# A graph layer with attention on one NeuronCore: a fifth gather buffer, block 0's messages during the setup, and 1 / sqrt by Newton's steps on VectorE

## The chip, the cores and the metric

The program runs on one core of a Trainium2 chip. The metric is the device time of one execution in microseconds; before the change it is 1334.2 us, the median of 8 runs (1331.74 to 1335.88). A profile is one such execution with every instruction's start, duration and semaphores recorded. PE is TensorE, with its weight loads shown as PEld; DVE is VectorE, ACT ScalarE, POOL GpSimd, SP SyncE.

## The reference, cut to what matters

There are 8192 nodes of 256 features, in groups of 32, and 131072 edges sorted by their target, with 64 attributes each. All data is fp32.

```python
ea  = edge_attr @ w_e + b_e                       # 131072 x 256
msg = relu(x[src] + ea)
agg = segment_sum(msg, dst, num_segments=8192)    # dst is sorted
h_local = bn(relu((x + agg) @ w1 + b1) @ w2 + b2 + x)
# attention with 4 heads of 64 inside each group of 32 nodes
h_attn  = bn(softmax(q k^T / 8) v @ out_w.T + out_b + x)
out = h_local + h_attn
out = bn(out + relu(out @ m_w1 + m_b1) @ m_w2 + m_b2)
return layernorm(x + out)                         # (z - mean) / sqrt(var + 1e-5)
```

## The kernel before, in words

**Edges** go in 128 blocks of 1024. A block's source rows come by `gather` (L133): eight indirect DMAs of 128 rows of 1 KB each, issued by POOL (L138), into one buffer `xs` of a ring of four. The first 20 blocks (`NX`) read x itself, and a matmul with `sel` and `be` adds the edge bias (L462). Later blocks read `xb`, a copy of x with the bias added; the copy is made in 13 pieces while the first blocks run: load `xp` (L551), add `be` on DVE (L556), store (L557), all loads and stores from SP's queue. Indices of blocks 0 and 1 are loaded directly (`srcd`, L64); those of the others are turned by PE in the setup (L196) and copied to `srci` (L197).

Per block, `edge_products` (L454) multiplies the attributes, transposed on DVE (L164), by `w_e` into two PSUM tiles `pe` (L468). `edge_messages` (L479) adds the gathered rows on DVE (L488) and applies Relu on ACT (L489). `edge_hot` (L494) makes one-hot rows of the target's place; `edge_sums` (L508) sums messages by a matmul with them; `edge_place` (L526, L536) puts the sums into the transposed nodes `xT` of the right chunk.

**Nodes** go in 16 chunks of 512. `attention_front` loads x (L279), transposes it (L286) and makes q and k (L297). `attention_back` makes v (L311), the scores (L328, into the same two PSUM tiles as the edge products), a softmax on DVE and ACT (L344 to L355, Exp at L346), the values (L363) and the output projection (L375). `dense` runs four matmul layers (all at L394, called from L401, L404, L410 and L419), transposes back (L431), and ends with the layer norm: statistics per row (L436, L437), Sqrt on ACT (L439), a reciprocal (L442), the scaling (L444) and the store (L447). Chunks 0 to 13 run as one `dense` call each; 14 and 15 are cut in five smaller calls.

**What sets the order.** PE's order is written out by the program. The main loop takes blocks in pairs up to `TAIL` = 104: gather for two blocks ahead, products and messages of the first, sums of the pair before, a share of node work, products and messages of the second, placing, another share, one-hots, and the rest. `Work.run` hands out the node work: four streams (BACK, FRONT, DENSE, DENSE2) of generators that yield the cost they put on PE; a stream goes on when its `ready` condition holds. A pair has the budget 2 x `PER` (2 x `PER_X` for the first 20 blocks), given in shares of 0.2, 0.2 and 0.6. BACK may make scores only when no products wait for their messages. From block 104 on a second loop places each step by expected times: block i's gather is taken to come at 11.5 + 10.06 (i + 1) us. DVE's and ACT's order is that of the program up to block 26 (`NV`), then a scheduler's. POOL issues the gathers in block order; before a gather its buffer must have been read by the messages of four blocks earlier.

Of the kernel before, what the change touches and what calls it, by code (L numbers as in the profile page):

```python
# [9 lines left out]
FP = mybir.dt.float32  # L10
I32 = mybir.dt.int32
# [13 lines left out]
NH = 4  # L25
# [20 lines left out]
LN_EPS = 1e-5  # L46
REST = -1.0
# [6 lines left out]
def gnn_kernel(ctx: ExitStack, tc: tile.TileContext, x, src, dst, edge_attr, w, out):  # L54
# [37 lines left out]
    be = const.tile([P, TJ, C], FP, name="be")  # L92
# [40 lines left out]
    def gather(b):  # L133
        xs = epool.tile([P, NH, TJ, C], FP, name="xs", tag="xs", bufs=4)
        for h in range(NH):
            for j in range(TJ):
                idx = srcd[:, b * NH + h, j : j + 1] if b < ND else srci[:, b, h * TJ + j : h * TJ + j + 1]
                nc.gpsimd.indirect_dma_start(  # L138
                    out=xs[:, h, j, :],
                    out_offset=None,  # L140
                    in_=x if b < NX else xb[:, :],
                    in_offset=bass.IndirectOffsetOnAxis(ap=idx, axis=0),
                )
        xs_of[b] = xs
# [9 lines left out]
    load_edges(0)  # L154
    gather(1)
    load_edges(1)
# [8 lines left out]

    with tc.tile_pool(name="setup", bufs=1) as sp:


        srci_r = npool.tile([P, BE], I32, name="srci_r", tag="y")
        dsti_r = npool.tile([P, BE], I32, name="dsti_r", tag="h1")  # L170
        nc.sync.dma_start(srci_r, src.rearrange("(s e) -> s e", s=NB))
        nc.sync.dma_start(dsti_r, dst.rearrange("(s e) -> s e", s=NB))
        for h in range(NH):
            nc.scalar.dma_start(we[h * QR : (h + 1) * QR], w["w_e"].rearrange("(i d) c -> d i c", d=QR))
        nc.scalar.dma_start(be, w["b_e"][None, None, :].to_broadcast([P, TJ, C]))
        in_r = npool.tile([P, 3 * KC, C], FP, name="in_r", tag="m1")
        out_r = npool.tile([P, KC, C], FP, name="out_r", tag="vn")
        nc.scalar.dma_start(in_r, w["in_w"].rearrange("(o p) c -> p o c", p=P))
# [4 lines left out]
        nc.scalar.dma_start(out_r, w["out_w"].rearrange("(o p) c -> p o c", p=P))  # L183
        for b in range(2):
            edge_transpose(b)
            load_edges(b + 2)
# [6 lines left out]
        for h in range(NH):  # L193
# [3 lines left out]
            nc.vector.tensor_copy(srci[:, :, h * TJ : (h + 1) * TJ].rearrange("p s j -> p j s"), ps)  # L197

# [78 lines left out]
    def attention_front(n0, st, pool, bank):  # L277
        xn = st["xn"] = pool.tile([P, TN, C], FP, name="xn", tag="xn", bufs=4)
        nc.sync.dma_start(xn, x[ds(n0, CH), :].rearrange("(t p) c -> p t c", p=P))  # L279
        yield REST  # L280
# [102 lines left out]

    def dense(n0, st, pool, bank, t_a=0, t_z=TN, own=("h1", "m1", "zT", "y", "")):
# [54 lines left out]
        nc.scalar.activation(rstd[:, :nt], mv[:, :nt, 1], AF.Sqrt, bias=eps_t)  # L439
        st["dense"] = t_z == TN  # L440
        yield 0.9 * part
        nc.vector.reciprocal(rstd[:, :nt], rstd[:, :nt])  # L442
# [7 lines left out]

    chunk = [{} for _ in range(NCH)]
    pe_of, msg_of, oh_of, newest = {}, {}, {}, {}

    def edge_products(b):  # L454

        eaT = eaT_of.pop(b).rearrange("p t m r -> p t (m r)")
        pes = [bank2().rearrange("p i (j c) -> p i j c", j=TJ) for _ in range(2)]
        pe_of[b, 0], pe_of[b, 2] = pes
        quarter = [slice(h * QR, (h + 1) * QR) for h in range(NH)]
        if b < NX:  # L460
            for h, rows in enumerate(quarter):
                nc.tensor.matmul(  # L462
                    pes[h // 2][:, h % 2], sel[rows, :], be[rows], start=True, stop=False, skip_group_check=True
                )
        for j in range(TJ):
            for i in range(ED // QR):
                for h, rows in enumerate(quarter):
                    nc.tensor.matmul(  # L468
                        pes[h // 2][:, h % 2, j, :], eaT[rows, j * ED // QR + i, :], we[rows, i, :],
                        start=(b >= NX and i == 0), stop=(i == 1), skip_group_check=True,  # L470
                    )

    def next_edges(b):
        if b < NB:
            edge_transpose(b)
        if b + 2 < NB:
            load_edges(b + 2)

    def edge_messages(b):  # L479

        xs = xs_of.pop(b)
        msg = msg_of[b] = epool.tile([P, NH, TJ, C], FP, name="msg", tag="msg", bufs=3)
        n = 2 if b < NB - 1 else 1
        for h in range(0, NH, 2):
            pe = pe_of.pop((b, h))
            for u in range(0, 2, n):
                hs = slice(h + u, h + u + n)
                nc.vector.tensor_add(msg[:, hs], pe[:, u : u + n], xs[:, hs])  # L488
                nc.scalar.activation(msg[:, hs], msg[:, hs], AF.Relu)  # L489

    def edge_hot(b):

        oh = oh_of[b] = epool.tile([P, TB, WN], FP, name="oh", tag="oh", bufs=2)
        nc.vector.tensor_tensor(  # L494
            oh,
            iota_n[:, None, :WN].to_broadcast([P, TB, WN]),
            rel[:, b, :, None].to_broadcast([P, TB, WN]),
            ALU.is_equal,
        )

    def edge_sums(blocks):

        pw = pps.tile([P, 2, C], FP, name="pw", tag="pw", bufs=1)
        for i, b in enumerate(blocks):
            msg, oh = msg_of.pop(b), oh_of.pop(b)
            for j in range(TJ):
                for h in range(NH):
                    nc.tensor.matmul(  # L508
                        pw[h * WN : (h + 1) * WN, i, :], oh[:, h * TJ + j, :], msg[:, h, j, :],
                        start=(j == 0), stop=(j == TJ - 1), skip_group_check=True,  # L510
                    )
        n = len(blocks)
        ws = epool.tile([P, 2, C], FP, name="ws", tag="ws", bufs=2)
        newest["ws"] = nc.scalar.copy(ws[:, :n], pw[:, :n]).ins  # L514
        oh2 = epool.tile([P, 2, WB], FP, name="oh2", tag="oh2")
        for i, b in enumerate(blocks):
            nc.vector.tensor_scalar(oh2[:, i, :], iota_n, wrow[:, b : b + 1], None, ALU.is_equal)
        return blocks, ws, oh2

    def edge_place(blocks, ws, oh2):  # L520

        l2 = pps.tile([P, KC, C], FP, name="l2", tag="pw", bufs=1)
        last = len(blocks) - 1
        for i in range(last + 1):
            for k in range(KC):
                nc.tensor.matmul(  # L526
                    l2[:, k, i * NPB : i * NPB + WB], ws[:, i, k * P : (k + 1) * P], oh2[:, i, :],
                    start=(i == 0 and k == 0), stop=(i == last), skip_group_check=True,
                )
        n = blocks[0] * NPB - WL  # L530
        end = n + last * NPB + WB
        for c in range(max(n, 0) // CH, (min(end, N) - 1) // CH + 1):
            assert chunk[c]["v"]
            a, z = max(n, c * CH), min(end, (c + 1) * CH)
            xT = chunk[c]["xT"][:, :, a - c * CH : z - c * CH]
            newest["xT"] = nc.vector.tensor_add(xT, l2[:, :, a - n : z - n], xT).ins  # L536
# [330 lines left out]
```

## Time and profile before

| what | value |
|---|---|
| median of 8 runs, lowest, highest | 1334.2, 1331.74, 1335.88 us |
| the profiled execution's own time | 1332.63 us |
| its span, first to last instruction | 1330.8 us |
| mean granted TensorE clock | 0.966 |
| POOL: first gather starts, last ends | 4.13, 1299.66 us |
| ACT: table loads | 22 of 1283 ns (11 before Sqrt, 10 before Exp, 1 at the start) |
| DVE: additions for xb (L556) | 13, 18.4 us |
| DMA | 207 MB, 156 GB/s on average |

How to read it: the page gives each engine's busy time as a share of the span. Matmuls are pipelined, so a PE share of 90% does not say that PE sets the end. Groups of instructions carry, after the first bar, busy time and mean duration of one in ns, and after the second the idle time just before them with what ended it; "issue" means that nothing in the profile held the engine. In a timeline a row has start, duration, engine, line, operation, what is written and read, and how many instructions are merged. The table by stage gives for each stretch its length, then busy time of PE, PEld, DVE, ACT and POOL with counts, the granted clock, the DMA share and GB/s.

### The profile page before, as it was taken

Reading aid. Unit: us, or ns where it says so; the run is one execution under the profiler, and the core shown is the slowest. Engines: PE = TensorE matmul, PEld = TensorE weight load, DVE = VectorE, ACT = ScalarE, POOL = GpSimd, SP = SyncE. Lnnn points to the kernel's source line nnn. Section 1 sums busy time; section 2 is a strip of 40 time slices with the busy share of each in tenths; the row PEclk is TensorE's granted clock in tenths of the full one; section 3 lists DMA queues with packets and bytes.
Section 4 is the critical chain, followed back from the end, with each engine's and each line's share of the span. In section 5 each row is a group of like instructions: output and inputs, shape, how many; then the busy total and the mean of one; then the engine's idle time right before and its main releaser. Section 6 shows DMA issues by size and latency. Waiting matters only on the chain.

```text
span 1330.8 us, 24244 instructions
## 1 busy us (share of the span) xinstructions
PE 1210.1 (91%) x9683; PEld 738.8 (56%) x9683; DVE 784.9 (59%) x1347; ACT 586.3 (44%) x840; POOL 984.7 (74%) x1032
## 2 busy tenths in 40 slices
PE   4998989998989989899998979999897998979987
PEld 3565645555555545555555545555555555545755
DVE  5676655746565564746646564665746467464754
ACT  2434344454535444454535435453544536343433
POOL 6777777777777777777777777777777777777770
PEclk9998989999999989999898999999998999989989
DMA  8887654545454454545545454554545445454540
GB/s 272 273 264 275 187 174 137 153 144 162 136 150 140 136 151 138 162 135 145 152 135 155 137 151 139 142 156 136 158 131 158 132 137 160 127 145 130 161 122 30
DMA packets 92882, 207.23 MB, mean 156 GB/s; under 512 B 20798, under 2 KB 39772, under 8 KB 91996
## 3 DMA queue, kind: packets, MB, share of 16 engines
q0 software_dynamic: 49152, 134.28, 35.3%
q1 hardware_dynamic: 41388, 69.76, 16.2%
q10 hardware_dynamic: 2224, 1.58, 0.5%
q8 instruction: 78, 1.28, 0.4%
q14 instruction: 40, 0.33, 0.1%
HBM read 188.77 MB, written 16.78 MB: 154 GB/s over the span
## 4 chain that ended last, share of the span: by engine, by line
PE 59%; POOL 11%; DVE 11%; issue 8%; DMA 5%; ACT 5%; DVEq 0%; ACTq 0%; SPq 0%; POOLq 0%
PE at L394 19%; PE pe L468 14%; POOL xs L138 11%; PE at L297 7%; PE pw L508 6%; DVE msg L488 4%; PE l L526 4%; PE at L375 4%; PE at L311 3%; DMA xs<-xb,srci 2%; ACT msg L489 1%; ACT pr L338 1%; DMA xs<-in_x_dram,srci 1%; PE at L363 1%; DVE eaT L164 1%
## 5 line engine op out<-in xcount | busy, mean ns | idle before, releaser
L138 POOL DMA_INDIRECT xs<-xb,srci x864 | 824.3, 954 | 263.4 <-issue 244.8
L489 ACT ACTIVATE msg<-msg 128x1024 f32<-128x1024 f32 (+1 forms) x258 | 270.0, 1050 | 456.1 <-DVE msg L488 451.0
L488 DVE TENSOR_TENSOR msg<-pe,xs 128x1024 f32<-128x1024 f32 (+1 forms) x258 | 305.0, 1196 | 153.1 <-PE pe L468 70.1
L468 PE MATMUL pe<-we,eaT 32*128 32x256 f32 x4096 | 291.3, 402 | 31.4 <-DVE msg L488 17.5
L468 PEld LDWEIGHTS pe<-we,eaT 32*128 32x128 f32 x4096 | 222.5, 193 | 121.6 <-issue 68.7
L138 POOL DMA_INDIRECT xs<-in_x_dram,srci x144 | 143.9, 999 | 43.9 <-issue 40.2
L164 DVE STREAM_TRANSPOSE eaT<-ea 128x512 f32<-128x512 f32 x128 | 90.1, 704 | 105.1 <-PE pe L468 102.4
L508 PE MATMUL pw<-msg,oh 128*32 128x256 f32 x2048 | 127.7, 385 | 0.0
L394 PE MATMUL at<-hA,mw 128*128 128x512 f32 (+2 forms) x304 | 123.8, 533 | 2.6 <-ACT oT L370 1.8
L297 PE MATMUL at<-xT,inT 128*128 128x512 f32 x256 | 124.8, 613 | 0.2 <-ACT xT L287 0.2
L394 PE MATMUL at<-m,mw 128*128 128x512 f32 (+2 forms) x304 | 117.3, 528 | 0.3
L508 PEld LDWEIGHTS pw<-msg,oh 128*32 128x32 f32 x2048 | 59.1, 110 | 61.8 <-issue 26.6
L526 PE MATMUL l<-oh,ws 128*128 128x160 f32 x512 | 90.6, 316 | 2.8 <-ACT ws L514 2.8
L526 PEld LDWEIGHTS l<-oh,ws 128*128 128x128 f32 x512 | 73.3, 192 | 28.2 <-issue 21.3
L394 PEld LDWEIGHTS at<-hA,mw 128*128 128x128 f32 x304 | 53.2, 190 | 52.1 <-issue 42.0
L394 PEld LDWEIGHTS at<-m,mw 128*128 128x128 f32 x304 | 54.4, 190 | 48.3 <-issue 44.2
L297 PEld LDWEIGHTS at<-xT,inT 128*128 128x128 f32 x256 | 47.2, 193 | 53.7 <-issue 48.2
L394 PE MATMUL at<-h,w 128*128 128x512 f32 (+2 forms) x152 | 67.0, 567 | 7.7 <-ACT h L401 6.7
L394 PE MATMUL at<-xT,w 128*128 128x512 f32 (+2 forms) x152 | 66.8, 577 | 6.6 <-DVE xT L536 6.6
L300 ACT ACTIVATE qk<-at,vec 128x512 f32<-128x512 f32 x64 | 43.4, 681 | 56.9 <-PE at L297 56.8
L419 DVE SCALAR_TENSOR_TENSOR zT<-at,s,zT 128x512 f32<-128x512 f32 (+2 forms) x38 | 25.2, 664 | 66.0 <-PE at L394 65.4
L378 DVE SCALAR_TENSOR_TENSOR hA<-at,s,hA 128x512 f32<-128x512 f32 x32 | 24.0, 750 | 67.7 <-PE at L375 67.7
(107 smaller groups left out, 1209.3 us busy)
## 6 DMA issues: line engine op xcount, KB each, us to landing
ea<-in_edge_attr_dram SPq DMA_DIRECT2D x128, 256.0 KB
xs<-xb,srci POOLq DMA_INDIRECT x864
xn<-in_x_dram SPq DMA_DIRECT2D x16, 512.0 KB
out_dram<-y SPq DMA_DIRECT2D x14, 512.0 KB
xp<-in_x_dram SPq DMA_DIRECT2D x10, 512.0 KB
xb<-xp SPq DMA_DIRECT2D x10, 512.0 KB
xp<-in_x_dram SPq DMA_DIRECT2D x3, 1024.0 KB
xb<-xp SPq DMA_DIRECT2D x3, 1024.0 KB
```

Of the source, the lines that this page charges most:

```text
L138: nc.gpsimd.indirect_dma_start(out=xs[:, h, j, :], out_offset=None, in_=x if b < NX else xb[:, :], in_offset=bass.IndirectOffsetOnAxis(ap= ...
L164: nc.vector.transpose(eaT, ea.rearrange("p (m t d) -> p t m d", m=EQ, d=QR))
L297: nc.tensor.matmul(ps, inT[:, k, o * P : (o + 1) * P], xT[:, k, :], start=(k == 0), stop=(k == KC - 1))
L300: nc.scalar.activation(qk[:, o, :], ps, AF.Identity, bias=v_("in_b", o))
L311: nc.tensor.matmul(ps[:, (t - t0) * C : (t - t0 + 1) * C], xT[:, k, t * P : (t + 1) * P], inT[:, k, 2 * C :], start=(k == 0), stop=(k == K ...
L375: nc.tensor.matmul(ps, outT[:, k, o * P : (o + 1) * P], oT[:, k, :], start=(k == 0), stop=(k == KC - 1))
L394: nc.tensor.matmul(ps, wt[:, k, o * P : (o + 1) * P], act[:, k, :], start=(k == 0), stop=(k == nk - 1))
L468: nc.tensor.matmul(pes[h // 2][:, h % 2, j, :], eaT[rows, j * ED // QR + i, :], we[rows, i, :], start=(b >= NX and i == 0), stop=(i == 1), ...
L488: nc.vector.tensor_add(msg[:, hs], pe[:, u : u + n], xs[:, hs])
L489: nc.scalar.activation(msg[:, hs], msg[:, hs], AF.Relu)
L508: nc.tensor.matmul(pw[h * WN : (h + 1) * WN, i, :], oh[:, h * TJ + j, :], msg[:, h, j, :], start=(j == 0), stop=(j == TJ - 1), skip_group_ ...
L526: nc.tensor.matmul(l2[:, k, i * NPB : i * NPB + WB], ws[:, i, k * P : (k + 1) * P], oh2[:, i, :], start=(i == 0 and k == 0), stop=(i == la ...
```

## The change: a fifth buffer, a new setup order, Newton's steps, and the planner's numbers

Seven things change.

1. `xs` has five buffers in place of four. The bias tile `be` holds one row of 256 in place of two, and is broadcast where it is read.
2. In the setup all loads but the first index loads go by SP's queue: indices, edges of block 0, `w_e`, edges of block 1, the bias, targets, twelve vectors, `in_w`, x of chunk 0, `out_w`, x of chunk 1. Before, `w_e`, the bias, `in_w` and `out_w` were issued by ACT, and x came later.
3. Block 0's products, its next edges and its messages are made inside the setup, after the source indices are turned and ahead of the transposes of `in_w`; the main loop then leaves them out for block 0.
4. In `dense` calls of a full chunk (14 of them) 1 / sqrt(var + eps) is made on DVE: half the argument, a first guess by a shift and a subtraction on the bits as integers, and three Newton steps of three operations. The smaller calls keep Sqrt and the reciprocal. The reciprocal moves ahead of the yield.
5. `PER` is 5.2 (5.1), `PER_X` 4.4 (4.2).
6. From block 26 on the shares of a pair are 0.35, 0.2 and 0.45.
7. A flag `calm`: BACK makes scores only in a pair's last share, in which it also has the first turn, or after the main loop.

Functions for edges, and `chunk`, are also moved up in the text so that the setup can call them; their bodies are the same but for `be`.

```diff
+RSQ = 0x5F3759DF - (1 << 22) - (1 << 31)
-    be = const.tile([P, TJ, C], FP, name="be")
+    be = const.tile([P, C], FP, name="be")
-        xs = epool.tile([P, NH, TJ, C], FP, name="xs", tag="xs", bufs=4)
+        xs = epool.tile([P, NH, TJ, C], FP, name="xs", tag="xs", bufs=5)
...
         for h in range(NH):
             nc.vector.tensor_copy(
...
+        for b in range(2):
+            edge_transpose(b)
+            load_edges(b + 2)
+        edge_products(0)
+        next_edges(2)
+        edge_messages(0)
...
+    def rsqrt(r, var, pool, own):
+        b = pool.tile([P, 2, TN], FP, name="half", tag="half" + own)
+        t = b[:, 1, : r.shape[1]]
+        b = b[:, 0, : r.shape[1]]
+        nc.vector.tensor_scalar(b, var, LN_EPS, 0.5, ALU.add, ALU.mult)
+        nc.vector.tensor_scalar(r.bitcast(I32), b.bitcast(I32), 1, None, ALU.arith_shift_right)
+        nc.vector.tensor_scalar(r.bitcast(I32), r.bitcast(I32), -1.0, float(RSQ), ALU.mult, ALU.add)
+        for _ in range(3):
+            nc.vector.tensor_mul(t, r, r)
+            nc.vector.tensor_mul(t, t, b)
+            nc.vector.scalar_tensor_tensor(r, t, 1.5, r, op0=ALU.subtract, op1=ALU.mult)
...
-        nc.scalar.activation(rstd[:, :nt], mv[:, :nt, 1], AF.Sqrt, bias=eps_t)
+        if nt == TN:
+            rsqrt(rstd[:, :nt], mv[:, :nt, 1], pool, own[4])
+        else:
+            nc.scalar.activation(rstd[:, :nt], mv[:, :nt, 1], AF.Sqrt, bias=eps_t)
+            nc.vector.reciprocal(rstd[:, :nt], rstd[:, :nt])
         st["dense"] = t_z == TN
         yield 0.9 * part
-        nc.vector.reciprocal(rstd[:, :nt], rstd[:, :nt])
...
-    PER = 5.1
-    PER_X = 4.2
+    PER = 5.2
+    PER_X = 4.4
...
-(not pe_of or not s.get("v") or s.get("scores"))
+(work.calm and not pe_of or not s.get("v") or s.get("scores"))
...
-            edge_products(b)
-            next_edges(b + 2)
-            edge_messages(b)
+            if b:
+                edge_products(b)
+                next_edges(b + 2)
+                edge_messages(b)
...
-            work.run(0.2 * per)
+            work.run((0.2 if b < NV else 0.35) * per)
...
-            work.run(0.6 * per)
+            work.calm, work.turn = True, BACK
+            work.run((0.6 if b < NV else 0.45) * per)
+            work.calm = False
```

## The prediction

> **What bounds the kernel now.** I read the page first, then POOL's timeline, then the block-by-block distance between a gather and its messages, last the tail.
>
> ```profile
> span 1330.8 us, 24244 instructions
> ...
> PE 1210.1 (91%) x9683; PEld 738.8 (56%) x9683; DVE 784.9 (59%) x1347; ACT 586.3 (44%) x840; POOL 984.7 (74%) x1032
> ...
> L138 POOL DMA_INDIRECT xs<-xb,srci x864 | 824.3, 954 | 263.4 <-issue 244.8
> ```
>
> PE has the largest share, but POOL is the pace. Its 1024 gathers (864 here, 144 and 16 in other rows) are busy 954 ns each, and the idle time in front of each, some 0.305 us, is "issue": nothing that another engine could end. In POOL's timeline the first starts at 4.13 and they follow each other every 1.25 us to the last:
>
> ```profile
> 1296.20 0.95 POOL L138 DMA_INDIRECT xs<-xb,srci  x1 [0.30 <-issue]
> 1297.45 0.95 POOL L138 DMA_INDIRECT xs<-xb,srci  x1 [0.30 <-issue]
> 1298.71 0.95 POOL L138 DMA_INDIRECT xs<-xb,srci  x1 [0.30 <-issue]
> ```
>
> An unhindered gather is 0.947 us, so the step is 1.252, and 1024 of them 1282. From 4.13 that gives 1286; the last in fact ends at 1299.66. The missing 13.7 us are inside single gathers that took longer. I set each of them beside DVE's timeline; the largest look like this:
>
> ```profile
> 60.81 2.59 POOL L138 DMA_INDIRECT xs<-in_x_dram,srci  x1 [0.30 <-issue]
> 63.71 0.94 POOL L138 DMA_INDIRECT xs<-in_x_dram,srci  x1 [0.30 <-issue]
> ...
> 60.31 3.41 DVE L556 TENSOR_TENSOR xp<-xp,be 128x2048 f32<-128x2048 f32 x2
> ```
>
> A gather that starts while DVE adds two SBUF tensors ends only some 0.8 us after that addition. Six under L556 hold 6.7 us of the 13.7; most of the rest started under softmax (L345, L351) or one-hot (L494) operations with two SBUF inputs.
>
> So span = 4.1 (start) + 1282 (gathers) + 13.7 (hindered) + 31.2 (tail after the last gather). A change in PE's, ACT's or DVE's middle gains only if it reaches one of these four.
>
> **Does POOL ever wait for a buffer?** Counting gathers by eight gives the blocks. With four buffers, gather b+4 needs block b's messages. The closest pair is block 14, messages ending 185.89, and gather 18, starting 191.86: 6.0 us to spare; elsewhere it is 6.6 to 27. No gather waits for one.
>
> **The tail.** In 31.2 us there are 7.8 from the last gather's end to its messages at 1307.44, then 23.4 to the end. In blocks 87 and 59 the messages began 0.1 and 0.7 us after the block's last gather, so most of the 7.8 is PE's lateness. This distance is 10.0 us at block 104, 14.4 at 114, 18.2 at 118, 13.4 at 121, 8.3 at 124, 7.8 at 127. The table by stage says why:
>
> ```profile
> 1160.00:1190.00 30.00, 22.81 (x200) 14.00 (x202) 19.80 (x40) 10.56 (x18) 22.79 (x24) 0.89 0.42 121
> 1190.00:1220.00 30.00, 29.42 (x220) 16.50 (x216) 14.91 (x22) 14.07 (x20) 22.68 (x25) 1.00 0.52 148
> 1220.00:1250.00 30.00, 30.00 (x256) 20.36 (x248) 20.57 (x41) 10.41 (x16) 22.69 (x25) 1.00 0.51 150
> ```
>
> The first busy column is PE. It loses 7 us around the last softmax (1160 to 1190), then is full for 60 us and cannot catch up. PE work taken out of this stretch comes off the tail.
>
> **The change part by part.**
>
> *Fifth buffer, smaller bias tile.* Removes a wait that never comes: 0. It is cover should messages run later (10 us more).
>
> *Setup order and block 0 first.* The index loads still lead both queues, so the first gather stays at 4.1. On SP's queue the edge weights, in_w and node loads now stand in one line with the twelve vector loads; in_w comes behind them, about 10 us later than its old issue at 6.51. PE's transposes waited for xn until 26.55 and 29.27 anyway. ACT no longer issues seven loads; its first work came at 11.39. The xp and weight loads queue behind on SP (at 21.80 and 24.26 now); xp is first read at 60.31, so 30 us cover that. Block 0's products and messages fill that time: PE gains one block early (1.9 us of L468). Nothing of this reaches POOL: block 2's gather (24.51) needs only the index transposes, which stay first on PE. Gather 20 needs the last xb store; it is issued at 193.62 and the gather starts at 212.26 after its usual 0.31, so a store later by several us costs nothing. Bounds: -0.5 to +2, from these gaps; value 0.
>
> *Newton's steps.* Removed: 14 Sqrt at 297 ns, 14 reciprocals at 174 ns, and 20 of 22 table loads at 1283 ns: in the built order one load stays at the start and one before the first partial chunk. ACT loses 25.7 + 4.2 = 29.9 us. Added: 14 x 12 = 168 DVE operations on 128x4. No such chain is in the trace; the nearest rows are L252 (two tensors, 152 ns), L254 (220 ns), and the dependent pair L273, L274, 0.17 us start to start. At 0.17 a chain is 2.0 us and all 14 are 28, so DVE goes from 785 to some 810 us. Where a load stood in front of messages it delayed them (ACT, 1184 to 1188):
>
> ```profile
> 1184.47 1.06 ACT L489 ACTIVATE msg<-msg 128x1024 f32<-128x1024 f32 x1 [4.48 <-DVE msg L488]
> 1185.55 1.28 ACT L439 ACT_TABLE_LOAD   x1
> 1186.84 0.30 ACT L439 ACTIVATE rstd<-mv,eps_t 128x4 f32<-128x4 f32 x1
> ```
>
> In the middle both are covered by POOL: 0. Behind a chain on DVE stand the next messages and edge transposes, and PE waits for those; a chain replaces a reciprocal that waited 1.3 us for the load, so I count +0.7 us of lateness per chunk, covered too. In the tail the load above goes, but one comes back near block 121, up to 1.3 us on ACT's message path: 0 net.
>
> What is not covered is POOL: 9 of a chain's 12 operations may have two SBUF inputs. Lower end 0 (a chain's data is 4 elements a partition). Upper end: a chain hinders like one L556 pair of 2.3 us (0.22 to 0.77 us over the three pairs): 14 x 0.5 = 7. L494, 0.41 us long, hindered 17 gathers of its 128 operations and took 1.67 us, 13 ns an operation; 126 operations at up to that is 1.6. They are shorter: I take 0.5.
> The Trainium skill, SBUF — State Buffer, section "SBUF: two separate sides", speaks against this part: a Vector operation with two SBUF inputs takes the port pair that GpSimd shares for the whole instruction. The rows above agree for long operations. By the rule read to the letter, each of the 126 could hold a gather up to its own length of 0.15 us, and some 20 gathers fall on chains: an estimate of 3 us in place of 0.5.
>
> *Planner.* PER 5.1 to 5.2, PER_X 4.2 to 4.4, more of a pair's share between its products after block 26, scores only after both products. From the two built orders I counted PE's matmuls that remain after a block's edge products. After block 104 the new order has 2 fewer of L297, 8 of L311 and 16 of L328: 1.9 + 3.5 + 2.0 = 7.4 us by their rows. After 110 it is 4, 2 and 2 fewer of L297, L375 and the 512-wide L394 (0.95 us each): 7.6 us. After 116 six: up to 5.7. After 120 eight 256-wide ones (0.48 each): 3.8. From block 124 on both orders are the same. The price is earlier: 6 to 7 us more PE work between blocks 26 and 104, where PE idled some 14 us of each 240 and messages often waited only for their gather. The last scores also stand one block earlier (112, not 113). So PE arrives at block 120 with 3.8 us less to do while the gathers keep their times. I take the lateness at 127 from 7.8 to about 4: -3.7. Bounds: -6.5 (messages right behind the landing) to +3 (the returning table load plus a chain of 2 us, on the path).
>
> **Sum.** Start 0, gathers 0, hindered +0.5, tail -3.7: -3.2. The profiled span becomes 1327.6 and its run 1332.6 - 3.2 = 1329.4. That run is 1.6 below the median of 1334.2; from the median the forecast is **1331.0**.
>
> **Rivals.**
> 1. *The tail does not move* (no change). For it: PE at half clock cost time in just this stretch (0.89 in 1160 to 1190), and DVE's longer chains sit in the same in-order queue as the messages. Against it: the orders differ by 3.8 us at block 120. Gain 0 to 2: 1332 to 1335, centre 1334.2 + 0.5 = 1334.7.
> 2. *Newton's chains hold the gathers* (slower). Place: each full chunk's end, POOL. Price 7 us: 1334.2 - 3.7 + 7 = 1337.5. It decides when hindered time exceeds 13.7 + 3.7 + 2.7 = 20.1 us, i.e. 0.46 us a chain. For it: the L556 rows; against it: 4 elements are soon read.
> 3. *Messages follow the landing* and fewer gathers meet xp's additions: -6.5 - 1.5: 1326.
> 4. *The change does not do what it says*: the fifth buffer frees nothing. I hold this for that part in any case; it costs nothing.
>
> **How the numbers follow.** A measurement of this kernel tells about 0.2% (2.7 us) from no change. Forecast 0.38, rival 3 0.12: faster 0.50. Rival 1: same 0.32. Rival 2 0.13 and a late xb store or later PE 0.05: slower 0.18. The range takes in rivals 1 to 3 up to their centres: 1326 to 1337.5.
>
> **What would show it.** Right: last gather ending within 2 us of 1299.7, hindered time 12 to 17 us; messages of block 127 starting 3 to 5 us behind the last gather; 2 table loads; ACT near 556, DVE near 810. Wrong: long gathers over the chains on 128x4; a gather idle behind a message or an xb store; a distance at 124 again of 8 us or more.

## The result, and the profile after

The changed kernel takes **1338.8 us**, the median of 12 runs (1335.44 to 1343.53); the kernel before takes 1334.1 on the same chip (32 runs). The ratio is 1.0036, 95% interval 1.0028 to 1.0044: slower by 4.8 us, where 3.2 us less was forecast. The profiled execution took 1342.3 us, its span is 1340.4 and the mean granted clock 0.962.

First the page of the changed kernel: the span, the engines' busy time, and the group of gathers with its busy time, mean ns of one, and idle time before.

```profile
span 1340.4 us, 24339 instructions
...
PE 1208.7 (90%) x9683; PEld 734.7 (55%) x9683; DVE 810.3 (60%) x1501; ACT 555.4 (41%) x806; POOL 983.6 (73%) x1032
...
L139 POOL DMA_INDIRECT xs<-xb,srci x864 | 823.0, 953 | 263.4 <-issue 248.4
```

DVE has risen from 784.9 to 810.3 and ACT fallen from 586.3 to 555.4, as forecast to within a microsecond. PE and POOL have kept their busy time, the gathers their 953 ns and their "issue" gaps. So the loss is in no engine's busy time.

Next POOL's timeline of the changed kernel: start, duration, instruction, and the idle time before it. The last gather, and the worst encounter with an addition for xb:

```profile
57.60 3.40 DVE L588 TENSOR_TENSOR xp<-xp,be 128x2048 f32<-128x2048 f32 x2
57.91 2.77 POOL L139 DMA_INDIRECT xs<-in_x_dram,srci  x1 [0.30 <-issue]
```

```profile
1296.27 0.95 POOL L139 DMA_INDIRECT xs<-xb,srci  x1 [0.30 <-issue]
1297.52 0.95 POOL L139 DMA_INDIRECT xs<-xb,srci  x1 [0.30 <-issue]
```

The last gather ends at 1298.47, 1.2 us **earlier** than before. Hindered time, counted as in the prediction, is 12.3 us (13.7 before), and all of it that began under one of Newton's operations is below 0.1 us. POOL's side went as forecast; all that was lost came after the last gather: 41.9 us to the end, where 31.2 were before. Block 127's messages start 18.1 us behind the last gather, not 7.8.

The table by stage of the changed kernel (length, then PE, PEld, DVE, ACT and POOL busy with counts, granted clock, DMA share, GB/s) for the three stages shown of before:

```profile
1160.00:1190.00 30.00, 20.33 (x192) 12.78 (x193) 20.70 (x51) 10.28 (x18) 22.68 (x25) 0.83 0.50 146
1190.00:1220.00 30.00, 30.00 (x201) 15.36 (x200) 15.21 (x23) 12.14 (x17) 22.69 (x25) 1.00 0.47 133
1220.00:1250.00 30.00, 27.71 (x218) 19.00 (x217) 20.58 (x49) 10.84 (x17) 22.68 (x25) 0.94 0.49 143
```

PE's loss around the last softmax has grown from 7 to 9.7 us. PE is then full for 30 us, as before, but idles 2.3 us of the next 30, in which it was full before. But the lateness is much older. This is the distance from a block's last gather to its first message addition, in us, from the traces of four kernels (the two in the middle belong to the experiments):

| block | before | Sqrt back (e1) | Newton in 7 to 13 only (e10) | after |
|---|---|---|---|---|
| 0 | 21.6 | 4.5 | 4.8 | 4.8 |
| 26 | 10.2 | 4.3 | 4.3 | 5.8 |
| 58 | 6.0 | 4.3 | 4.3 | 4.7 |
| 66 | 3.1 | 6.6 | 6.6 | 10.7 |
| 82 | 1.6 | 7.9 | 14.8 | 17.3 |
| 100 | 13.2 | 5.2 | 14.5 | 20.0 |
| 112 | 4.8 | 1.7 | 9.9 | 13.7 |
| 113 | 7.1 | 4.0 | 17.6 | 21.1 |
| 120 | 14.9 | 8.2 | 20.7 | 24.5 |
| 127 | 7.8 | 7.8 | 16.0 | 18.1 |

Up to block 58 the changed kernel is ahead or at most 4 us behind. Then it goes up in steps, by blocks 66, 82 and 113, and from block 82 on it is never below 11 us. (e1's profiled execution, 1331.3 us, was the slowest of its six; its usual distances are probably smaller, but no trace shows them.)

### The profile page after: what moved, and what is told of

Read it like the earlier page. It is cut to its first block, busy times and chain, and to the rows that moved or that the text cites. A ratio compares the mean times of both kernels' runs of the same rounds, so it can differ in the third digit from the quotient of the medians.

```text
span 1340.4 us, 24339 instructions
## 1 busy us (share of the span) xinstructions
PE 1208.7 (90%) x9683; PEld 734.7 (55%) x9683; DVE 810.3 (60%) x1501; ACT 555.4 (41%) x806; POOL 983.6 (73%) x1032
## 5 line engine op out<-in xcount | busy, mean ns | idle before, releaser
L182 PE MATMUL pe<-we,eaT 32*128 32x256 f32 x4096 | 295.3, 405 | 34.5 <-DVE msg L202 31.8
L510 PE MATMUL at<-m,mw 128*128 128x512 f32 (+2 forms) x304 | 120.3, 537 | 6.1 <-ACT m L526 5.3
L400 PE MATMUL at<-xT,inT 128*128 128x512 f32 x256 | 121.3, 600 | 3.4 <-DVE y L550 3.1
L510 PE MATMUL at<-xT,w 128*128 128x512 f32 (+2 forms) x152 | 70.7, 600 | 30.4 <-DVE xT L250 29.9
L510 PE MATMUL at<-h,w 128*128 128x512 f32 (+2 forms) x152 | 62.8, 537 | 2.8 <-ACT h L517 2.7
L478 PE MATMUL at<-oT,outT 128*128 128x512 f32 x128 | 60.9, 602 | 1.9 <-ACT oT L473 1.9
L414 PE MATMUL at<-inT,xT 128*128 128x256 f32 x256 | 60.2, 382 | 1.8 <-ACT qk L403 1.8
```

Of the source, the lines that this page charges most:

```text
L182: nc.tensor.matmul(pes[h // 2][:, h % 2, j, :], eaT[rows, j * ED // QR + i, :], we[rows, i, :], start=(b >= NX and i == 0), stop=(i == 1), ...
L400: nc.tensor.matmul(ps, inT[:, k, o * P : (o + 1) * P], xT[:, k, :], start=(k == 0), stop=(k == KC - 1))
L414: nc.tensor.matmul(ps[:, (t - t0) * C : (t - t0 + 1) * C], xT[:, k, t * P : (t + 1) * P], inT[:, k, 2 * C :], start=(k == 0), stop=(k == K ...
L478: nc.tensor.matmul(ps, outT[:, k, o * P : (o + 1) * P], oT[:, k, :], start=(k == 0), stop=(k == KC - 1))
L510: nc.tensor.matmul(ps, wt[:, k, o * P : (o + 1) * P], act[:, k, :], start=(k == 0), stop=(k == nk - 1))
```

## The experiments

Of the seven changes, those that reach DVE's queue or PE's order behind the setup are Newton's steps (4) and the planner (5 to 7). My theory after the result was that Newton's chains, put in DVE's in-order queue ahead of messages and xT additions, make PE wait (N); the rival, that the planner's new numbers do it (P). All times are medians. Each group ran beside the kernel before on its own chip, so kernels are compared by their ratios to it; where I turn a difference of two ratios into us, I multiply by 1334, and it is good to some 3 us.

| run | kernel | us | before there | ratio, 95% interval |
|---|---|---|---|---|
| e1_sqrt | after, Sqrt for all chunks | 1326.4 | 1332.6 | 0.9948, 0.9930 to 0.9966 |
| e2_plan | after, planner of before | 1334.7 | 1332.6 | 1.0008, 0.9995 to 1.0020 |
| e3_both | after, Sqrt and planner of before | 1333.4 | 1332.6 | 1.0002, 0.9993 to 1.0012 |
| e4_per | after, PER 5.1 and 4.2 | 1342.4 | 1332.6 | 1.0073, 1.0059 to 1.0086 |
| e5_onestep | after, one Newton step | 1333.0 | 1332.6 | 1.0004, 0.9990 to 1.0019 |
| e6_beside | Sqrt, chain into an unread tile | 1340.8 | 1332.6 | 1.0061, 1.0044 to 1.0078 |
| e7_none | neither Sqrt nor chain | 1327.9 | 1332.6 | 0.9965, 0.9951 to 0.9978 |
| e8_behind | Newton, chunk's end behind messages | 1331.3 | 1332.6 | 0.9996, 0.9981 to 1.0011 |
| e9_first7 | Newton in chunks 0 to 6 | 1326.8 | 1333.3 | 0.9957, 0.9941 to 0.9974 |
| e10_last7 | Newton in chunks 7 to 13 | 1340.8 | 1333.3 | 1.0061, 1.0043 to 1.0078 |
| e11_behind_sqrt | Sqrt, chunk's end behind messages | 1330.2 | 1333.3 | 0.9970, 0.9955 to 0.9985 |
| e12_sqrt_per | Sqrt, PER 5.1 and 4.2 | 1335.1 | 1333.3 | 1.0017, 0.9998 to 1.0037 |
| e17_four | Newton in chunks 9, 10, 11, 13 | 1331.0 | 1332.9 | 0.9987, 0.9976 to 0.9999 |
| e18_sqrt_per53 | Sqrt, PER 5.3 | 1336.5 | 1332.9 | 1.0025, 1.0016 to 1.0034 |

### Newton or planner: e1, e2, e3, e4

```diff
# e1: never true, so every chunk takes Sqrt and the reciprocal
-        if nt == TN:
+        if nt > TN:
# e2, in short (e3 is e1 and e2 together; e4 is the first two lines alone)
+    PER = 5.1
+    PER_X = 4.2
+    work.run(0.2 * per) ... work.run(0.6 * per)
+    scores when: not pe_of or not s.get("v") or s.get("scores"); no first turn for BACK
```

e1: 

> The changed kernel with Sqrt on ACT and the reciprocal for every chunk, nothing else different. Theory N (Newton's chains, some 2.4 us each and drawn out among the softmax, stand in DVE's in-order queue ahead of messages and xT additions): the 4.7 us come back, 1334 us or a little less, block 127's messages 8 to 10 us behind the last gather. Theory P (the planner's numbers put softmax and layer norm in front of the messages and give each pair more node work than it can carry): 1337 to 1339, messages still 16 to 18 us behind; 22 table loads in either case. If neither is enough alone: between, about 1336.5.

e2: 

> The changed kernel with the planner of before: PER 5.1 and 4.2, shares 0.2, 0.2, 0.6 throughout, scores allowed whenever no products wait, no first turn for BACK. Newton, the setup and five buffers stay. Theory P: the loss goes, 1332 to 1334, distance at block 127 7 to 9 us. Theory N: the loss stays, 1338 to 1339, distance 16 to 18 us. In both the last gather ends within 1.5 us of 1298.5.

e3: 

> Sqrt on ACT and the planner of before; only the five buffers, the small bias tile, the setup order and block 0's early messages stay. Both theories: 1332.5 to 1334.5, the time of before, distance at 127 7 to 9 us and the early lead (distance near 5 us at block 0) gone by block 40, as POOL does not see it. A rival S (the setup itself or the fifth buffer costs the time): 1338 or more.

e4: 

> The changed kernel with PER 5.1 and PER_X 4.2 again; the new shares, calm, BACK's first turn and Newton stay. If the size of the budget is what piles up (theory P by its sum): 1334 to 1335, and the distance at blocks 60 to 104 stays under 12 us. If it is the place of the work in the pair (theory P by its order) or Newton: 1337 to 1339, with the steps up at blocks 60, 68 and 74 as before.

With Sqrt back the kernel is not level with before but **faster than both**, 0.9948. So the new planner is worth 0.54% (e1 against e3), some 7 us, and Newton takes 0.88% (e1 against after), 11.7 us. N holds, but not alone: under the old planner the same Newton costs 0.06% (e2 against e3), within the intervals. P as I put it falls: the planner alone gains, and a smaller budget (e4) makes the kernel with Newton slower still. By their numbers only e3 fell where a theory put it; e1 is faster, e4 slower than either theory said, and e2 (1334.7, distance 12.7 us at block 127) lies between the two. In e3 that distance is 11.2 us, not 7 to 9.

e4 has a partner in e12 below, which is the same kernel with Sqrt: with the old budget, but the new shares and `calm`, Newton costs 0.56% (1.0073 against 1.0017, good to 0.24), 7.5 us. So it is not the larger budget alone that makes the chains dear. What remains of the planner are the shares, `calm` and BACK's first turn; no run tells these apart.

e3 is the first three changes (buffers and bias tile, setup, block 0 first), with the reciprocal moved ahead of the yield, without the rest: 1.0002. They are worth nothing, though block 0's messages come 17 us sooner (4.5 in place of 21.6).

What a chain does to DVE's queue is plainest at block 82. DVE's timeline of the kernel with Sqrt (e1), from the layer norm's statistics to the messages:

```profile
850.61 0.39 DVE L552 BATCH_NORM_STATS2 st<-y 128x6 f32<-128x256 f32 x1
...
851.40 0.65 DVE L447 TENSOR_REDUCE mx<-pr 128x16 f32<-128x512 f32 x1
...
852.09 0.69 DVE L448 TENSOR_TENSOR pr<-pr,mx 128x512 f32<-128x512 f32 x1
852.70 0.17 DVE L559 RECIPROCAL rstd<-rstd 128x4 f32<-128x4 f32 x1
852.90 1.49 DVE L563 TENSOR_SCALAR y<-y,mv,rstd 128x256 f32<-128x256 f32 x4
854.32 1.21 DVE L202 TENSOR_TENSOR msg<-pe,xs 128x1024 f32<-128x1024 f32 x1
```

The same stretch of the changed kernel:

```profile
854.61 0.69 DVE L448 TENSOR_TENSOR pr<-pr,mx 128x512 f32<-128x512 f32 x1
855.22 0.16 DVE L492 TENSOR_SCALAR half<-mv 128x4 f32<-128x4 f32 x1
855.42 0.17 DVE L493 TENSOR_SCALAR rstd<-half 128x4 int32<-128x4 int32 x1
...
856.11 0.68 DVE L452 TENSOR_REDUCE sm<-pr 128x16 f32<-128x512 f32 x1
...
857.11 0.69 DVE L454 TENSOR_TENSOR pr<-pr,sm 128x512 f32<-128x512 f32 x1
...
860.46 0.71 DVE L458 STREAM_TRANSPOSE bd<-pr 32x512 f32<-32x512 f32 x1
861.20 0.16 DVE L498 SCALAR_TENSOR_TENSOR rstd<-half,rstd 128x4 f32<-128x4 f32 x1
...
861.91 1.56 DVE L563 TENSOR_SCALAR y<-y,mv,rstd 128x256 f32<-128x256 f32 x4
863.39 2.34 DVE L202 TENSOR_TENSOR msg<-pe,xs 128x1024 f32<-128x1024 f32 x2
```

From L448 to the message addition are 2.2 us with Sqrt and 8.8 us with Newton. The chain itself is 12 operations of some 0.16 us, a new one every 0.20 us; but the scheduler, which puts DVE's order together ahead of time, filled the chain with the rest of the softmax and all four bd transposes, and the messages stand behind the chain's end. With Sqrt the same operations come after the first message addition. Only two of the 14 chains are filled like this, with seven other operations each: this one and the one ahead of block 113. The other twelve have none to two. PE's timeline of e1 and then of the changed kernel shows who waits (PE's order is the same in both):

```profile
855.58 0.70 PE L182 MATMUL pe<-we,eaT 32*128 32x256 f32 x4 [1.47 <-DVE msg L202]
858.10 2.00 PE L182 MATMUL pe<-we,eaT 32*128 32x256 f32 x28 [1.82 <-DVE msg L202]
```

```profile
864.75 4.91 PE L182 MATMUL pe<-we,eaT 32*128 32x256 f32 x32 [8.11 <-DVE msg L202]
```

PE waits 8.11 us in one piece in place of 3.3 in two, and the 32 matmuls then take 4.91 us, not 2.70 (at half the granted clock, see the last section). PE's longest waits between 600 and 1300 us, of e1 and of the changed kernel (us in all, times, longest):

```profile
PE pe L182 <- DVE msg L202: 25.5, 18, 3.5
PE at L510 <- DVE xT L250: 15.5, 9, 4.6
```

```profile
PE pe L182 <- DVE msg L202: 26.2, 17, 8.1
PE at L510 <- DVE xT L250: 23.2, 9, 8.4
```

The number of waits is about the same; a few have become long. Of PE's idle stretches of 4 us or more between 600 and 1300 the changed kernel has four (6.7 us at 623, 8.1 at 865, 5.0 at 958, 8.4 at 1181), e1 one of 4.6. By the table by stage PE is busy 633.75 of these 700 us in the changed kernel and 642.00 in e1: 8.2 us less. A lower granted clock takes 3.1 us more (last section). The two profiled executions differ by 11.0 us (1342.3 and 1331.3): that is where the time went.

### Length, place, or the missing Sqrt: e5, e6, e7, e8

```diff
# e5
-        for _ in range(3):
+        for _ in range(1):
# e6
+        nc.scalar.activation(rstd, ..., AF.Sqrt, bias=eps_t); nc.vector.reciprocal(rstd, rstd)
+        if nt == TN:
+            rsqrt(spare_r, mv[:, :nt, 1], pool, own[4])
# e7
-            rsqrt(rstd[:, :nt], mv[:, :nt, 1], pool, own[4])
+            nc.vector.tensor_scalar(rstd[:, :nt], mv[:, :nt, 1], LN_EPS, 0.5, ALU.add, ALU.mult)
# e8: rsqrt, scaling and store of a full chunk become a function end(), which
#     the next edge_messages calls after its additions
+        with tc.issue_after(add.ins):
+            while late:
+                late.pop(0)()
```

e5: 

> The changed kernel with one Newton step in place of three: 6 operations a chunk instead of 12 (the result of 1 / sqrt is then only good to some thousandths). DVE keeps the order of the changed kernel, only the chain is 1.2 us shorter. Theory L (the chain's length on DVE is what costs; with Sqrt the kernel was 12 us faster): half the loss goes, 1331 to 1334. Theory O (the order: messages queued behind softmax and bd transposes where the chain is drawn out, at blocks 74, 82 and 113): 1336 to 1339. Busy time of DVE near 795 in both.

e6: 

> Sqrt and reciprocal for every chunk as in the kernel with Sqrt (1326), and Newton's 12 operations beside them, into a tile that nobody reads. DVE carries as much as in the changed kernel, ACT as much as before, the scaling does not wait for the chain. By the built order the DVE work ahead of the messages of block 82 is 4 us and of block 113 4.5 us shorter than in the changed kernel, elsewhere 0.7 us longer. Theory L: 1337 to 1341. Theory O: 1328 to 1331. A third, A (the missing Sqrt on ACT shifts the softmax): 1326 to 1327.

e7: 

> The changed kernel with 1 / sqrt left out for the full chunks: one DVE operation writes half the variance in its place. No chain, no Sqrt, two table loads. Theory L: as with Sqrt or up to 2 us better, 1324 to 1327; that would also be all that 20 table loads off ACT are worth. Theory A: 1330 or more.

e8: 

> The changed kernel, but the whole end of a full chunk (three Newton steps, scaling, store) is queued on DVE behind the next block's message additions. PE's order and DVE's amount of work are those of the changed kernel. By the built order the DVE work ahead of block 74's, 82's and 113's messages falls by 3.9 us each, that of most chunks by 3.9 us, and 3.9 us more stands ahead of blocks 30 and 60. Theory O: 1327 to 1331, distance at block 127 7 to 11 us. Theory L: 1336 to 1339.

PE's order is the same in e1, e5, e6, e7, e8 and after. e7 says that the 32 us of ACT time in Sqrt and table loads (587.5 in e1, 555.2 in e7) are worth nothing that can be measured: 0.9965 without them, 0.9948 with them. A falls with it, though 1327.9 us is 0.9 above L's range too. e6 says the reverse: all that work stays on ACT, the scaling does not wait for the chain, and it is at least as slow as with Newton, 1.0061 against 1.0036; so the operations themselves cost, not their result. e5 takes away half the chain and gives back 0.32% of 0.88%. These are for L. But e8, with DVE's work unchanged and only moved, gives back 0.40% and lands at the upper end of where O put it (1331.3 us, 8.7 us at block 127). By the traces it takes 3.5 to 4.1 us from in front of 12 blocks' messages and puts about as much in front of the next block's each time, not only at blocks 30 and 60. So both the amount of DVE work ahead of messages and its place count; the next runs ask at which messages.

### Which chunks: e9, e10, e17

```diff
# in short: a test that n0 is a fixed number is left out
-        if nt == TN:
+        if nt == TN and n0 < 7 * CH:                     # e9;  >= 7 * CH in e10
+        if nt == TN and n0 // CH in (9, 10, 11, 13):     # e17
```

e9: 

> The changed kernel with Newton's steps in chunks 0 to 6 only and Sqrt with the reciprocal in 7 to 13. From block 60 on DVE's built order is that of the kernel with Sqrt throughout (1326). Theory B (before block 60 the chains fall where PE has spare time; what counts is the work ahead of messages from there to the end): 1326 to 1328. A rival E (every chain costs the same, 12 / 14 = 0.85 us): 1332.

e10: 

> The opposite: Sqrt in chunks 0 to 6, Newton in 7 to 13. From block 60 on DVE's order is that of the changed kernel. Theory B: 1335 to 1339, distance at block 127 15 to 18 us. Rival E: 1332. If both halves are near 1326 alone, the loss needs both: the lateness built up by the first meets the second.

e17: 

> Newton only in chunks 9, 10, 11 and 13, Sqrt elsewhere, as e13, whose chip ran the kernel before in 2061 us and so cannot be set beside the other runs. Theory D (the price lies where a chain drags softmax and transposes ahead of the messages, chunks 7, 8 and 12): 1326 to 1329. Theory L (each late chain costs by its length): 1334 to 1335.

Seven chains in the first half cost 0.09%, 1.2 us, within the intervals; seven in the second half 1.13%, 15 us. In the traces e9's chains stand ahead of blocks 22 to 66, e10's of blocks 74 to 119. B holds, and E falls. But e10 came out 1.8 us above B's range, and with half the chains it is no faster than the changed kernel with all 14 (1.0061 against 1.0036): the parts do not simply add up. The table by stage of e9 and then of e10, in stretches of 160 us:

```profile
760.00:920.00 160.00, 148.15 (x1177) 90.46 (x1178) 94.71 (x161) 74.77 (x106) 121.31 (x127) 0.96 0.48 143
920.00:1080.00 160.00, 150.25 (x1169) 88.30 (x1167) 93.39 (x159) 74.65 (x102) 121.23 (x128) 0.97 0.48 144
1080.00:1240.00 160.00, 147.45 (x1180) 88.18 (x1180) 99.86 (x183) 68.84 (x101) 121.13 (x128) 0.98 0.50 147
```

```profile
760.00:920.00 160.00, 143.46 (x1167) 88.07 (x1166) 95.32 (x180) 69.05 (x100) 121.03 (x128) 0.96 0.49 143
920.00:1080.00 160.00, 148.18 (x1169) 87.77 (x1168) 96.25 (x179) 69.24 (x96) 121.31 (x128) 0.98 0.49 145
1080.00:1240.00 160.00, 142.56 (x1109) 83.25 (x1108) 100.95 (x208) 60.58 (x90) 121.31 (x128) 0.96 0.48 142
```

The first busy column is PE: 4.7, 2.1 and 4.9 us less in e10, 11.7 together, with POOL the same to 0.3 us.

e17 lies between D and L: four late chains cost 0.39%, 5.2 us, so the other three (7, 8, 12) 0.74%, 9.9 us. "Only the three that drag" does not fit, and "each chain alike" (8.6 and 6.4) misses by some 3.5 us, where each difference is good to 3. These numbers are set against e10. Set against the changed kernel, 11.7 us less the 1.2 of e9, the three cost 5.3, and "each chain alike" (6.0 and 4.5) fits. So which chains are dear is not settled.

An account that fits the first reckoning is the DVE work that a chain puts ahead of message additions in the built order, counted with the durations of the rows: 2.2 us each for the four, 8.8 in all; 3.6, 7.2 and 6.6 for the three, 17.4 in all. (By e10's trace against e1's it is 1.9 to 2.2 and 3.4, 6.8 and 6.3; of the last two, 5.0 and 4.4 are then missing ahead of the next block's messages, so they are moved rather than added.) 5.2 / 8.8 = 0.59 and 9.9 / 17.4 = 0.57: by this each microsecond of DVE work set ahead of the messages cost a good half. One step in place of three takes away 7 x 1.2 = 8.4 us of it and gave 4.3 (0.51); in e6 19.5 us more cost 15.0 (0.77). With 3 us of doubt on each cost the likeness of these quotients shows little. It is an account of sizes, not a law: e8 and e11 do not keep to it.

### Can it be better still: e11, e12, e18

```diff
# e11: e1 with e8's end() behind the next block's additions
# e12: e1 with
+    PER = 5.1
+    PER_X = 4.2
# e18: e1 with
+    PER = 5.3
```

e11: 

> The changed kernel with Sqrt and the reciprocal, and with the whole end of a full chunk queued behind the next block's message additions. By the built order 1.7 us (reciprocal and scaling) leave the front of most late chunks' messages, 1.7 us come in front of blocks 30, 60 and 114. If DVE work ahead of late messages is the price: 1322 to 1326, a little under the kernel with Sqrt alone. If that kernel already has its messages right behind the landing: 1326, no difference.

e12: 

> Sqrt for every chunk and PER 5.1, PER_X 4.2; shares, calm, BACK's turn, setup and buffers stay as changed. If the larger budget is what the new planner's 7 us come from (less matmul work left behind block 104): 1330 to 1334. If shares and calm bring it: 1326 to 1328.

e18: 

> Sqrt for every chunk, PER 5.3, as e16, for the same reason. If what is left behind block 104 still sets the end: 1320 to 1325. If PE has no room left before block 104: 1327 to 1332.

None beats e1, and all three lie above what was expected. e12, at 1335.1 against 1330 to 1334, is nearest to the budget's side: the new shares and `calm` with the old budget bring nothing (1.0017 against 1.0002 in e3). e18, at 1336.5, lies above both of its ranges. e11 came to 1330.2, slower than e1 by 0.22% with intervals that overlap. Its DVE, ACT and PE at block 83, from the timeline:

```profile
865.11 1.60 DVE L567 TENSOR_SCALAR y<-y,mv,rstd 128x256 f32<-128x256 f32 x4
...
866.97 1.21 DVE L203 TENSOR_TENSOR msg<-pe,xs 128x1024 f32<-128x1024 f32 x1
...
868.22 1.06 ACT L204 ACTIVATE msg<-msg 128x1024 f32<-128x1024 f32 x1 [5.81 <-DVE msg L203]
...
869.18 0.67 ACT L477 ACTIVATE oT<-at,vec 128x512 f32<-128x512 f32 x1
...
869.90 0.66 PE L393 MATMUL at<-ident,xn 128*128 128x128 f32 x4 [2.22 <-ACT oT L477]
...
871.63 3.78 PE L514 MATMUL at<-xT,w 128*128 128x512 f32 x4 [1.07 <-ACT oT L477]
```

Pushed behind block 82's additions, the scaling now stands ahead of block 83's. Their Relu comes late on ACT, the copy `oT` waits behind it in ACT's queue, and PE waits 2.22 us for `oT`; its next four 512-wide matmuls take 3.78 us (granted clock 0.55 over 870 to 875 us), where e1's took 1.98 (1.00). The distance goes from 11.3 us at block 82 to 17.9 at 84 (e9: from 11.6 to 13.2). Work moved behind one message is ahead of the next.

PER 5.1 gave 1.0017, 5.2 0.9948, 5.3 1.0025. So the planner's gain is not simply that more is done early. At 5.3 PE is late from block 52 on (distance 19.9, against 11.6 in e1) and stays 12 to 24 us late to the end: the budget is more than PE can carry between two gathers. At 5.1 the distance at 120 is 22.0 us (8.2 in e1), with too much left behind block 104. That 5.2 is better than both by 0.7% was found by these runs, not derived.

### Four runs that tell little: e13 to e16

e13 is e17's kernel and e16 is e18's; e14 has Newton in chunks 7, 8 and 12 only, and e15 is e2 with six steps (each step turns the sign, so its 1 / sqrt has the wrong sign).

e13: 

> The changed kernel with Newton only in chunks 9, 10, 11 and 13; Sqrt elsewhere. By the built order each chain puts its own 2.2 us ahead of one message addition (blocks 91, 98, 107, 119) and moves nothing else there. Theory D (what costs is that the chain drags: the scaling, the softmax and the bd transposes all come ahead of the messages at three chunks): 1326 to 1329. Theory L (each late chain costs by its length, 14.4 us over seven): 1326.4 + 4 x 2.06 = 1334.6.

e14: 

> The complement in the second half: Newton only in chunks 7, 8 and 12, Sqrt elsewhere. By the built order the DVE work ahead of messages grows by 3.6 us at block 74, 7.2 at 82 and 6.6 at 113, more than the chain's 2.2. Theory D: 1335 to 1340, steps up of distance at 82 and 113. Theory L: 1326.4 + 3 x 2.06 = 1332.6.

e15: 

> The kernel with the planner of before and Newton (1334.7), with six steps in place of three: 21 operations a chunk, some 1.8 us more on DVE each, 25 us in all. If the smaller budget leaves PE time that takes up such delays: 1334 to 1337. If the earlier result was an accident of the order and length costs there as in the changed kernel: 1340 or more.

e16: 

> Sqrt for every chunk and PER 5.3 in place of 5.2 (PER_X 4.4). 5.1 gave 1335, 5.2 gave 1326. If what is left behind block 104 still sets the end: 1320 to 1325. If PE has no room left before block 104, so that the larger budget only moves lateness forward: 1327 to 1332.

They fell on a chip where the kernel before took 2061.4 us, and came to 2079.6, 2087.7, 2091.9 and 2041.4. There the gathers do not set the pace, by e13's page (busy time of the engines) and its POOL timeline:

```profile
PE 1465.1 (71%) x9683; PEld 843.8 (41%) x9683; DVE 795.2 (39%) x1391; ACT 585.9 (29%) x834; POOL 982.5 (48%) x1032
```

```profile
700.61 0.95 POOL L139 DMA_INDIRECT xs<-xb,srci  x1 [4.92 <-DVE msg L202]
```

DVE, ACT and POOL do their work in their usual time, PE needs 21% more, and gathers wait for messages even with five buffers. e13's mean granted clock is 0.828, against 0.962 in the changed kernel, which goes with PE's extra 256 us. But PE is also idle for 589 us in place of 132, about a third of it "issue". Why the clock was lower there and PE idle so long was not found. The runs answer nothing about a kernel paced by gathers; what e13 and e16 were to tell, e17 and e18 told. What e15 was to tell, why the old planner hides the chains, stays open.

## Why the prediction was wrong

**Start, gathers, hindered time: right.** First gather 4.10, last end 1298.47 (within 2 us of 1299.7), hindered 12.3 us (12 to 17 forecast). Newton's operations held gathers up by less than 0.1 us in all, below even the 0.5 taken; rival 2, whose price was 7 us, fell. The prediction set the Trainium skill's rule (SBUF — State Buffer, section "SBUF: two separate sides") against the 13 ns of L494's rows: read to the letter 3 us, measured under 0.1. 19 gathers began under one of the chains' operations, as many as estimated, and none lasted more than 0.002 us over the usual 0.947. The prediction's own rows agree: a hindered gather ended 0.82 us after the addition, so an operation has to reach some 0.13 us into a gather to lengthen it at all, and these last 0.16.

**Fifth buffer and setup: right.** In the changed kernel the message nearest to the gather four blocks later still had 3.0 us to spare (block 120), so four would have done. e3 puts all of the first edits at 1.0002.

**ACT and DVE totals: right.** 555.4 and 810.3 us, 2 table loads. e7, with ACT at 555.2 and 2 loads as well, is 0.7% faster than the changed kernel, so ACT's total does not decide.

**The step that failed** is in Newton's part: "+0.7 us of lateness per chunk, covered too". Both halves of it were wrong. The size: a chain puts 2.2 us, and in three chunks 3.6 to 7.2, ahead of the messages, since the order of DVE is made by a scheduler that fills some chains with softmax work. I had that built order before me and counted PE's matmuls in it, but not DVE's operations in front of each message. The cover: POOL's pace hides a late PE only as long as PE can make it up before the last gather. For the chains ahead of blocks 22 to 66 it does (e9: 1.2 us); for those ahead of blocks 74 to 119, with the new planner, it does not (e10: 15 us). I had noted that planner's price, "6 to 7 us more PE work between blocks 26 and 104", in the step below and did not put the two together. That this price is what takes the cover away is not shown: with the old budget the chains still cost 7.5 us (e4 against e12).

**The planner: right in sign, too small.** -3.7 us forecast from PE's remaining matmuls, -7.2 measured without Newton (e1 against e3). The profiled distances agree with the mechanism in part: 18.3 us at block 120 in e3, 8.2 in e1; but at block 127 e1 has 7.8 us like the kernel before, where about 4 was forecast. And the reasoning would have made PER 5.3 better yet, which is slower than before.

**The rivals.** Rival 1 named DVE's in-order queue as the danger and let it eat up at most the 3.7 us of gain; its place was right, its price a third of the 11.7. No rival of mine had the chain as a loss on PE's side, which is the one that came; a "later PE" had a chance of 0.05 with others, and no price.

Open are two things: why the old planner hides the chains (0.06%) although PE is idle about as long there between 600 and 1300 (53 to 55 us, 58 in e1) and the old budget alone does not (0.56%), and how much of 5.2's gain over 5.1 and 5.3 is the accident of what falls beside what.

## What to carry to other kernels

Moving work from an engine with time to spare onto an in-order queue that the pace-setter's feeder waits on can cost a multiple of what it frees: 30 us off ACT brought nothing, 28 us onto DVE cost 12. Before pricing such a move, read the built order of that queue and count what now stands ahead of each instruction that others wait for; a scheduler may fill a dependent chain of tiny operations with other work, as it did here in two of 14. And "covered" has to name the stretch in which the lateness is made up again. The same chains cost 0.06% under the old planner and 0.88% under the new one, so two edits of one change must be priced together.

## What the runs showed of the hardware

- A dependent chain of operations on 128x4 runs on DVE at 0.16 us each, one every 0.20 us; nine in twelve have two SBUF inputs, and still they hindered gathers by under 0.1 us over 14 chains, where an addition of 128x2048, 2.27 us long, lengthened a gather from 0.95 to 2.77 us.
- A change between Exp and Sqrt on ACT shows as one table load of 1.283 us; taking away 22 of e1's 24 changed the time by nothing that these runs could measure (e7 against e1).
- A wait of PE can be paid twice. The changed kernel's stages around the 8.11 us wait at block 82 (columns as above):

```profile
855.00:860.00 5.00, 1.64 (x32) 0.73 (x24) 4.75 (x17) 1.22 (x2) 3.81 (x4) 1.00 0.59 186
860.00:865.00 5.00, 0.25 (x2) 0.28 (x4) 4.91 (x11) 0.36 (x1) 3.79 (x4) 0.50 0.48 140
865.00:870.00 5.00, 5.00 (x33) 3.45 (x33) 2.52 (x4) 1.75 (x2) 3.80 (x4) 0.50 0.72 229
870.00:875.00 5.00, 4.58 (x49) 3.88 (x49) 2.85 (x7) 3.74 (x6) 3.79 (x4) 0.98 0.51 157
```

The granted clock falls to 0.50 in the wait and is there for the 5 us after it; e1, which waits 3.3 us in two pieces, keeps 1.00 there. But the length of the wait does not decide alone: e9 has almost the same two waits (1.41 and 1.82 us, e1 1.47 and 1.82) and gets 0.50 behind them, so that the 28 products behind the second take 3.78 us in place of 2.00. e1's stages, then e9's, with e9's products:

```profile
855.00:860.00 5.00, 2.60 (x32) 1.92 (x32) 4.99 (x9) 2.70 (x3) 3.78 (x5) 1.00 0.82 251
860.00:865.00 5.00, 3.97 (x47) 3.29 (x45) 4.94 (x8) 1.63 (x2) 3.78 (x5) 1.00 0.39 109
```

```profile
855.00:860.00 5.00, 2.29 (x36) 0.97 (x28) 4.96 (x11) 3.56 (x4) 3.78 (x5) 0.88 0.85 273
860.00:865.00 5.00, 4.49 (x31) 3.60 (x32) 4.93 (x9) 1.06 (x1) 3.78 (x5) 0.50 0.53 160
```

```profile
860.51 3.78 PE L182 MATMUL pe<-we,eaT 32*128 32x256 f32 x28 [1.82 <-DVE msg L202]
```

The Trainium skill (TensorE: Matmul & The Clock Gate, section "Part 1: The HAM clock gate (the "warmup" mystery)") says that the gate knows a half and a full rate and watches PE's recent activity, and these rows agree with it: in the traces of the changed kernel and e1 the granted clock is only ever 0.50 or 1.00, and 0.88 or 0.98 are means over a stage. Over 600 to 1300 us, in stages of 5 us, busy time times the missing share of the clock comes to 21.9 us for PE in the changed kernel and 18.8 in e1: 3.1 us, beside the 8.2 us of idle time.
